# Narrow heads of a latent network: VectorE in source order, returned rows asked for a step earlier, a bias product moved behind the first keys and values

## The chip, the cores and the metric

The kernel runs on one core of a Trainium2 chip. The metric is the device time of one execution in microseconds. The core's engines work side by side, each through its own queue of instructions: TensorE (in profile lines PE, with its weight loads as PEld) multiplies matrices into PSUM, VectorE (DVE) and ScalarE (ACT) work elementwise and empty PSUM, GpSimd (POOL) does small elementwise work and issues gathers, and SyncE (SP) issues most of the other transfers. Instructions of different engines are ordered only by waits on each other's results and by the reuse of buffers.

## The reference, cut to what matters

The reference is a network of four layers. `x` is 16 batches of 64 tokens with 256 features. Each layer adds a cross attention to a context of 1024 keys with 192 features, then a sequence mixer, then a feed-forward part, each on the normalized `x`. The change lies in the cross attention of the second layer, which has 16 heads of only 16 features each ("narrow heads"), and in how it takes over the result of the expert layer ahead of it:

```python
# first layer, feed-forward: two experts of eight for each token
top_w, top_i = top_k(softmax(xt @ gate_w.T), 2)
y = sum over e of comb[:, e] * swiglu(xt, w1[e], w2[e], w3[e])    # comb: top_w, or 0
x = x + y + swiglu(x, sw1, sw2, sw3)

# second layer, cross attention; h = 16 heads, dh = 16
xn = layernorm(x)
q = (einsum('bld,ed->ble', xn, Wq) + bq).reshape(b, l, h, dh)
kv = (einsum('bmc,ec->bme', ctx, Wkv) + bkv).reshape(b, m, h, 2 * dh)
k, v = kv[..., :dh], kv[..., dh:]
att = softmax(einsum('blhd,bmhd->blmh', q, k) / sqrt(dh), axis=2)
out = einsum('blmh,bmhd->blhd', att, v).reshape(b, l, d)
x = x + einsum('bld,ed->ble', out, Wo) + bo
```

## The kernel before, in words

The 1024 tokens lie in SBUF as eight tiles of 128 tokens (`xs`); tile i holds batches 2i and 2i + 1. A framework turns the Python program into one queue for each engine, puts in the waits, and hands out buffers from pools: a tag with `bufs=3` has three buffers that are used in turn, and a fourth allocation waits for the release of the first. As a rule a scheduler chooses the order of each queue by its own estimate of times. Inside `tc.manual_schedule(engines={...})` the engines named keep the order of the source instead.

The stage is `L1_xattn` (from line 867). Ahead of it, the expert layer has written its output rows to a DRAM tensor `ys`. For each token two rows have to be brought back, multiplied by their gates and added to `x`. `carry(i)` (line 1416) does that for tile i: two times it takes a buffer "back" (four of them), has GpSimd gather 128 rows of `ys` (`gather_rows`, line 1414), and has VectorE multiply and add them (line 1423).

`queries(i)` (line 899) is a generator in three steps. The first calls `carry(i)`, normalizes the tile (statistics on VectorE in `norm_tile`, lines 158 to 162, the power -1/2 on GpSimd, line 164, the normalized tile `o` on VectorE, line 904) and has GpSimd add the output bias to `xs` (line 905). The second transposes `o` on TensorE into `hT` (line 908; for tile 0 behind 18 warm-up products). The third computes the queries on TensorE, spreads them on VectorE into `qs` (line 916), and has SyncE copy `qs` to the other half of the partitions (line 921).

`keys_values(b)` (line 926) gives four pieces: keys (TensorE, lines 940 and 942; emptied from PSUM by VectorE, line 945, and ScalarE, line 946), values (lines 954 and 961, emptied through `evict`, line 61 on VectorE or line 63 on ScalarE in turn), keys, values. `biases()` (line 889) computes the row that holds the value bias times the output matrix, plus the output bias: two small VectorE operations (line 892), three products, and a ScalarE copy (line 895).

The loop (line 1039) goes over 64 steps, four groups g of two head pairs for each of 16 batches b. TensorE's order in a step is the source order: it transposes the two exponentiated score tiles `p` of the step before (`keys_first`, line 240) in four groups, whose results are copied from PSUM by VectorE (line 244) and ScalarE (line 242) in turn; then it computes the scores of this step (line 981 by way of line 68); then "early" work; then a piece of the next batch's keys or values; then a step of `queries`, where one is due; then the averages of the step before (line 991); then "late" work. Within `scores`, VectorE takes the maximum of each of the two score tiles (`nmx`, line 228, 128x1024) and ScalarE exponentiates them and sums the rows (line 230).

After the last group of a batch, `own_columns` (lines 1010 and 1011, VectorE, `ym`) picks the columns of each head out of the averages. One step later, as early work, `shares` (line 996) takes the reciprocal of the sums on VectorE (line 999), turns it with a small product on TensorE (line 1003), and ScalarE copies the result (line 1005). For every second batch `weigh` (line 1013) follows another step later, and `project` (line 1021) as late work one step after that.

All PSUM tiles named `misc` share three banks in this stage; the transposes of `p`, keys, values, `shares`, `weigh` and the queries all take theirs from there.

Order of the queues before: at the start (lines 1028 to 1033) TensorE and VectorE are in source order, with `biases()` first. In the loop (line 1034) only TensorE is; VectorE's, ScalarE's, GpSimd's and SyncE's order is the scheduler's.

## Time and profile before

| what | value |
|---|---|
| median of three runs | 2835.01 us (2834.1 to 2840.91) |
| the profiled execution's own time | 2835.53 us |
| its span | 2833.7 us, 46044 instructions |
| TensorE's mean granted clock over the span | 0.98 |
| the last product of the expert layer ends | 425.5 us after the span's start |
| first product of the narrow heads | 429.56 us |
| first scores of the loop | 466.9 us |
| last scores of the loop end | 944.5 us |

A profile row of a timeline gives the start in us, the length in us, the engine, the line, the operation with its tiles and shapes and how many instructions were merged into the row; in brackets stands the idle time ahead of it and what ended it. In a row of waits stand the engine, its tile and line, the engine, tile and line it waited for, and then the total in us, how often, and the longest. A busy share of TensorE is taken from modelled ends of its products, so that a full row does not mean that the array is at its peak. TensorE's granted clock is 1.00 or 0.50 in this trace.

### The profile page before, as it was taken

Reading aid. Unit: us, or ns where it says so; the run is one execution under the profiler, and the core shown is the slowest. Engines: PE = TensorE matmul, PEld = TensorE weight load, DVE = VectorE, ACT = ScalarE, POOL = GpSimd, SP = SyncE. Lnnn points to the kernel's source line nnn. Section 1 sums busy time; section 2 is a strip of 40 time slices with the busy share of each in tenths; the row PEclk is TensorE's granted clock in tenths of the full one; section 3 lists DMA queues with packets and bytes.
Section 4 is the critical chain, followed back from the end, with each engine's and each line's share of the span. In section 5 each row is a group of like instructions: output and inputs, shape, how many; then the busy total and the mean of one; then the engine's idle time right before and its main releaser. Section 6 shows DMA issues by size and latency. Waiting matters only on the chain.

```text
span 2833.7 us, 46044 instructions
## 1 busy us (share of the span) xinstructions
PE 2655.2 (94%) x18778; PEld 1948.1 (69%) x18778; DVE 1403.3 (50%) x2825; ACT 1004.2 (35%) x2114; POOL 311.5 (11%) x429
## 2 busy tenths in 40 slices
PE   7988998999999899989999999998999998998998
PEld 3666894666666688866666666896666665666777
DVE  3665125666666644233434342423344756658692
ACT  2332222555555431222222222122235445455330
POOL 1121323000000112310101000201001000000000
PEclk9999998999999999999999999999999999999999
DMA  9513862111100114801111112463113213121210
GB/s 266 152 53 131 311 245 64 30 27 32 34 28 24 42 38 176 306 25 47 59 58 55 45 49 80 160 239 108 51 49 93 85 48 97 56 76 31 61 45 8
DMA packets 78160, 253.77 MB, mean 90 GB/s; under 512 B 14079, under 2 KB 25882, under 8 KB 68218
## 3 DMA queue, kind: packets, MB, share of 16 engines
q1 hardware_dynamic: 58490, 165.00, 18.6%
q0 software_dynamic: 13312, 80.28, 7.9%
q10 hardware_dynamic: 6144, 5.51, 0.6%
q8 instruction: 149, 2.44, 0.4%
q14 instruction: 65, 0.53, 0.1%
HBM read 233.80 MB, written 14.81 MB: 88 GB/s over the span
## 4 chain that ended last, share of the span: by engine, by line
PE 39%; DVE 9%; ACT 3%; DMA 2%; issue 2%; SPq 1%; POOL 1%; ACTq 0%; DVEq 0%; POOLq 0%
PE sc L516 9%; PE ps_h L68 5%; PE misc L552 4%; PE halves L68 3%; PE ps_t L530 3%; PE misc L68 3%; PE halves L552 2%; PE gu L68 2%; PE misc L547 2%; PE halves L2156 2%; DVE x L2132 2%; DVE nmx L228 1%; PE halves L547 1%; PE po L68 1%; DMA rep<-dus 1%
## 5 line engine op out<-in xcount | busy, mean ns | idle before, releaser
L228 DVE TENSOR_REDUCE nmx<-sc 128x1 f32<-128x1024 f32 x264 | 311.9, 1219 | 221.7 <-PE sc L516 147.6
L230 ACT ACTIVATE p<-sc,nmx 128x1024 f32<-128x1024 f32 x264 | 294.3, 1115 | 308.5 <-DVE nmx L228 308.5
L516 PE MATMUL sc<-ctxT,qp 128*128 128x512 f32 (+1 forms) x1024 | 359.8, 606 | 0.0
L516 PEld LDWEIGHTS sc<-ctxT,qp 128*128 128x128 f32 (+1 forms) x1024 | 140.3, 191 | 156.5 <-issue 153.4
L530 PE MATMUL ps_t<-ident,p 128*128 128x128 f32 x1024 | 140.3, 279 | 39.4 <-ACT pT L533 16.8
L2122 ACT ACTIVATE da<-rep,al 128x252 f32<-128x252 f32 x256 | 115.9, 500 | 133.1 <-DVE x L2132 124.9
L530 PEld LDWEIGHTS ps_t<-ident,p 128*128 128x128 f32 x1024 | 115.6, 142 | 64.1 <-ACT pT L533 20.0
L2132 DVE TENSOR_TENSOR_SCAN x<-da,x 128x512 f32<-128x512 f32 x128 | 153.0, 1222 | 2.7 <-ACT da L2122 1.9
L240 PE MATMUL misc<-ident,p 128*128 128x128 f32 x1024 | 137.1, 279 | 7.2 <-ACT p L230 6.8
L533 ACT COPY pT<-ps_t 128x512 f32<-128x512 f32 x166 | 94.1, 587 | 121.4 <-PE ps_t L530 121.2
L240 PEld LDWEIGHTS misc<-ident,p 128*128 128x128 f32 x1024 | 110.1, 141 | 32.6 <-ACT p L230 15.4
L164 POOL TENSOR_TENSOR ln_rs<-ln_ve,nhalf 128x1 f32<-128x1 f32 x80 | 45.0, 568 | 680.6 <-DVE ln_ve L162 599.1
L552 PE MATMUL halves<-pT,ctx 128*128 128x256 f32 x512 | 119.6, 387 | 0.0
L552 PE MATMUL misc<-pT,ctx 128*128 128x256 f32 x512 | 119.1, 386 | 0.0
L242 ACT COPY pT<-misc 128x512 f32<-128x512 f32 x128 | 75.0, 586 | 109.2 <-PE misc L240 108.7
L68 PE MATMUL ps_h<-r,w 128*128 128x256 f32 x512 | 113.4, 381 | 0.0
L2128 DVE TENSOR_TENSOR x<-rep,bc_rep 128x512 f32<-128x512 f32 x128 | 84.9, 690 | 57.3 <-PE halves L2156 54.4
L244 DVE COPY pT<-misc 128x512 f32<-128x512 f32 x128 | 88.4, 690 | 39.7 <-PE misc L240 28.5
L68 PEld LDWEIGHTS ps_h<-r,w 128*128 128x128 f32 x512 | 96.6, 190 | 15.9 <-issue 2.5
L552 PEld LDWEIGHTS halves<-pT,ctx 128*128 128x128 f32 x512 | 95.0, 191 | 17.4 <-issue 5.6
L552 PEld LDWEIGHTS misc<-pT,ctx 128*128 128x128 f32 x512 | 94.6, 190 | 17.1 <-issue 5.5
L68 PE MATMUL gu<-dT,wa 128*128 128x128 f32 x792 | 94.1, 279 | 7.5 <-DVE dT L61 4.1
(506 smaller groups left out, 4626.1 us busy)
## 6 DMA issues: line engine op xcount, KB each, us to landing
ctx<-in_ctx SPq DMA_DIRECT2D x48, 768.0 KB
ctxT<-in_ctxT SPq DMA_DIRECT2D x48, 512.0 KB
w<-in_L2f_W SPq DMA_DIRECT2D x24, 1024.0 KB
rep<-dus SPq DMA_DIRECT2D x256, 64.0 KB
ctxT<-in_ctxT SPq DMA_DIRECT2D x16, 768.0 KB
ctxT<-in_ctxT SPq DMA_DIRECT2D x96, 128.0 KB
ys<-yb ACTq DMA_DIRECT2D x40, 128.0 KB
bc_rep<-bcs SPq DMA_DIRECT2D x32, 128.0 KB
```

The source lines that it names most:

```text
L68: self.nc.tensor.matmul(out, lhsT, rhs, start=n == 0, stop=n == len(pairs) - 1)
L228: self.nc.vector.tensor_reduce(nmx, sc, AX.X, ALU.max, negate=True)
L230: self.nc.scalar.activation(p, sc, AF.Exp, bias=nmx, accum_out=sums)
L240: self.nc.tensor.transpose(ps[:, u, :], p[:, at : at + 128], self.ident)
L244: self.nc.vector.tensor_copy(pT[:, 0:4, :], ps)
L516: nc.tensor.matmul(sc[u][:, bass.ts(kh, 512)], qp[n][par][rows, h : h + 2, :].rearrange("p h q -> p (h q)"), ctx[0][rows, at], start=n == ...
L530: nc.tensor.transpose(ps[:, t, :], p[:, at : at + 128], self.ident)
L533: nc.scalar.copy(to, ps)
L547: nc.tensor.matmul(o2[cols, :].rearrange("p (u q) -> p u q", u=2), ck[:, t, 128:], pT[:, t, :, cols], start=t == 0, stop=t == NK - 1,)
L552: nc.tensor.matmul(o, ck[:, t, :128], pT[:, t].rearrange("p u q -> p (u q)"), start=t == 0, stop=t == NK - 1)
L2122: nc.scalar.activation(da[:, g, :, 1:], now[j][:, 0, :].rearrange("p (b s) -> p b s", s=S)[:, :, 1:], AF.Exp, scale=al[:, col : col + 1],)
L2132: nc.vector.tensor_tensor_scan(flat, da.rearrange("p g b s -> p (g b s)"), flat, 0.0, ALU.mult, ALU.add)
```

## The change

Three things are changed.

1. The two blocks of fixed order become one, over the whole stage, and VectorE stays in it: in the loop too its queue has the order of the source.
2. `carry` is split. The new `asked(i)` issues the gathers of a tile and gives back a function that does the additions. `carry` calls both at once, as it did. `queries` becomes a generator of four steps: first the gathers alone, then additions, normalization and bias. For tiles 0, 1 and 2 the gathers are asked for at the start; for tiles 3 to 7 in the last step of the batch ahead of the one that adds them (b odd, g = 3).
3. At the start, keys and values of batch 0 come first; `biases()` follows them, then the second step of `queries(0)`, the next keys, the other two steps of `queries(0)`, and the last values.

```diff
         def queries(i):
-            self.carry(i)
+            add = self.asked(i)
+            yield
+            add()
             mv, rs = self.norm_tile(self.xs[:, i, :], 1e-5)
...
         with self.tc.manual_schedule(engines={mybir.EngineType.PE, mybir.EngineType.DVE}):
+            turns = [queries(i) for i in range(3)]
+            next(turns[0])
+            pieces = keys_values(0)
+            pieces[0]()
+            pieces[1]()
             biases()
-            for piece, turn in zip(keys_values(0), (None, *[queries(0)] * 3)):
-                piece()
-                if turn is not None:
-                    next(turn)
-        with self.tc.manual_schedule(engines={mybir.EngineType.PE}):
+            next(turns[0])
+            next(turns[1])
+            pieces[2]()
+            next(turns[0])
+            next(turns[0])
+            pieces[3]()
+            next(turns[2])
             held, work = None, {}
-            one, two = queries(1), queries(2)
+            _, one, two = turns
             ahead = (one,), (one, two), (one, two), (two,)
...
                     elif b % 2 == 0 and g < 3 and b // 2 + 2 < NT:
-                        if not g:
-                            ahead = queries(b // 2 + 2)
+                        next(ahead)
+                    elif b % 2 and g == 3 and b // 2 + 3 < NT:
+                        ahead = queries(b // 2 + 3)
                         next(ahead)
...
     def carry(self, i, room=None, tag="back", bufs=4):
+        self.asked(i, room, tag, bufs)()
+
+    def asked(self, i, room=None, tag="back", bufs=4):
         if self.routed is None:
-            return
-        for n, (at, g) in enumerate(zip(self.routed.at, self.routed.gates)):
+            return lambda: None
+        rows = []
+        for n, at in enumerate(self.routed.at):
             y = self.lp.tile([128, D], F32, tag=tag, bufs=bufs, name="back") if room is None else room[:, n, :]
             self.gather_rows(y, self.ys, at[:, i : i + 1])
-            self.nc.vector.scalar_tensor_tensor(
-                self.xs[:, i, :], y, g[:, i : i + 1], self.xs[:, i, :], ALU.mult, ALU.add
-            )
+            rows.append(y)
+        def add():
+            for y, g in zip(rows, self.routed.gates):
+                self.nc.vector.scalar_tensor_tensor(
+                    self.xs[:, i, :], y, g[:, i : i + 1], self.xs[:, i, :], ALU.mult, ALU.add
+                )
+        return add
```

## The prediction

> **What bounds the kernel now.** I read the page first (busy shares, chain of waits), then busy time by stretch, the waits, and last the timeline of single steps.

> ```profile
> PE 2655.2 (94%) x18778; PEld 1948.1 (69%) x18778; DVE 1403.3 (50%) x2825; ACT 1004.2 (35%) x2114; POOL 311.5 (11%) x429
> PE 39%; DVE 9%; ACT 3%; DMA 2%; issue 2%; SPq 1%; POOL 1%; ACTq 0%; DVEq 0%; POOLq 0%
> ```

> TensorE (PE) is busy 94% of the span and leads the chain. The change touches one stage of twelve, so what counts is whether TensorE waits there. By stretch (length, then busy time of PE, PEld, DVE, ACT, POOL, then TensorE's granted clock, DMA share, GB/s):

> ```profile
> 425.50:466.90 41.40, 28.98 (x109) 15.53 (x109) 18.91 (x58) 3.66 (x7) 23.51 (x31) 0.75 0.29 81
> 466.90:927.00 460.10, 459.12 (x4300) 289.07 (x4302) 300.18 (x402) 250.94 (x452) 4.97 (x8) 1.00 0.11 31
> 453.90:461.90 8.00, 0.07 (x2) 0.04 (x1) 5.37 (x18) 0.00 (x0) 6.43 (x9) 0.63 0.46 139
> 274.70:277.50 2.80, 0.04 (x1) 0.00 (x0) 0.42 (x1) 0.37 (x1) 1.26 (x4) 1.00 1.02 421
> 278.50:281.70 3.20, 3.20 (x17) 3.20 (x16) 0.42 (x1) 0.38 (x1) 0.00 (x0) 0.50 1.04 419
> 2252.90:2255.70 2.80, 0.05 (x4) 0.04 (x2) 2.80 (x5) 2.06 (x5) 0.00 (x0) 1.00 0.16 48
> 2256.00:2262.00 6.00, 6.00 (x51) 5.31 (x48) 0.00 (x0) 1.16 (x4) 0.00 (x0) 1.00 0.00 0
> ```

> The stage's start (425.5 to the first scores at 466.9) loses time; its loop (466.9 to 927) does not: 459.1 of 460.1 us busy. So the start can gain, and in the loop there is nothing to gain and every new wait counts in full. The last four rows are two pauses of TensorE elsewhere: after 2.8 us of rest the clock once fell to 0.50 and once did not. What the start waits for (total, times, longest):

> ```profile
> PE misc L940 <- DVE v L61: 7.9, 1, 7.9
> PE misc L68 <- DVE bv L892: 4.1, 1, 4.1
> ```

> The 7.9 us are keys of batch 1 waiting for a PSUM bank that VectorE (DVE) empties only after it has added and normalized tiles its scheduler drew forward. One step of the loop (start, length, engine, line):

> ```profile
> 522.32 0.20 DVE L999 RECIPROCAL r<-sums 128x8 f32<-128x8 f32 x1 [1.33 <-ACT p L230]
> ...
> 528.74 0.75 DVE L945 TENSOR_SCALAR kT<-misc,vecs 128x512 f32<-128x512 f32 x1 [0.57 <-PE misc L942]
> 529.79 0.48 DVE L1010 TENSOR_SCALAR ym<-o,own 128x256 f32<-128x256 f32 x1 [0.30 <-PE o L991]
> 530.40 0.69 DVE L244 COPY pT<-misc 128x512 f32<-128x512 f32 x1
> 531.00 0.48 DVE L1011 SCALAR_TENSOR_TENSOR ym<-o,own,ym 128x256 f32<-128x256 f32 x1
> 531.14 0.42 PEld L240 LDWEIGHTS misc<-ident,p 128*128 128x128 f32 x4 [0.20 <-DVE pT L244]
> 532.80 0.28 PE L68 MATMUL misc<-ident,r 64*8 64x64 f32 x4
> 532.95 2.36 DVE L228 TENSOR_REDUCE nmx<-sc 128x1 f32<-128x1024 f32 x2 [0.87 <-PE sc L68]
> 533.01 1.99 PE L954 MATMUL misc<-w,ctxT 128*128 128x256 f32 x8
> ```

> See two things. The reciprocal of `shares` ran at 522.3, ten microseconds before the product that reads it (532.80), ahead of the two maxima (532.95 to 535.31). And the fourth group of transposes (531.14) starts 0.05 us after VectorE's first copy of `p` ends: there are three PSUM banks, so that copy is on TensorE's path.

> **The change, part by part.** The order of the changed kernel's queues is known from its compiled form; the times are mine.

> *Start.* TensorE gets its first work (keys, values of batch 0) when the branch ends, about 428.4, not at 429.56. At full clock its work to the first scores is: bias 1.6 (half of 3.1), keys three times 2.97 (441.93 to 444.90), values twice 2.99 (518.51 to 521.50), warm-up 4.2, transposes and queries 1.4; together 22.1. Added waits: VectorE now has `bv` (two at 0.36) behind the copy of `v` (0.68), so the bias product waits 1.5; the `hT` copy 0.6; a bank 0.3. VectorE's chain for tile 0 hides behind keys and warm-up (7 us). The clock was 0.50 for 10.2 us in each of two falls; the first stays, with 3.4 us (another row's length) to 10.2 at half rate, costing 1.7 to 5.1; I take 3.4. First scores: 428.4 + 22.1 + 2.4 + 3.4 = 456.3 against 466.9. **Gain 10.5** (9 to 12). SP only swaps one `qs` copy with a context fetch that is needed a batch later: nothing.

> *Reciprocal behind the maxima.* In source order `scores` comes before `shares`, so the queue is maximum, maximum, reciprocal, in all fifteen batches that have a next one. The product, then the keys or values, averages and transposes behind it in TensorE's queue wait from 532.80 to 535.31 + 0.20 + 0.05 = 535.56: 2.75 us. Fourteen times 2.75; in the last batch, where TensorE waits 1.4 us for `p` anyway, 1.3. **Loss 39.8.**

> *Additions in the loop.* For tiles 3 to 7 VectorE now does, between `kT` and the copy: two additions 0.87, statistics 0.76, a wait for GpSimd's (POOL) power, normalization 0.45, both `ym`. The power stands in GpSimd's queue behind the next gathers that the freed buffers let go (tiles 0 to 5), as it already did once:

> ```profile
> 447.44 0.95 POOL L1414 DMA_INDIRECT back<-ys,route_at  x1 [0.30 <-issue]
> 448.42 0.58 POOL L164 TENSOR_TENSOR ln_rs<-ln_ve,nhalf 128x1 f32<-128x1 f32 x1
> 449.04 0.47 DVE L904 TENSOR_SCALAR o<-xs,ln_mv,ln_rs 128x256 f32<-128x256 f32 x1 [2.20 <-issue]
> ```

> From `kT`'s end, 529.4: first addition 529.9, two gathers with gaps 2.25 to 532.15, power 0.58, normalization to 533.2, `ym` twice to 534.3, copy to 535.0, fourth group 535.04 instead of 531.14: 3.9 us, three times (tiles 3, 4, 5). Without gathers (6, 7): 2.9, twice. For tiles 1 and 2, in batch 0 without `ym` and partly under the exponentials: 3.5 and 2.8. **Loss 23.8.** Everything later in the step waits with it. The gathers of the loop land over 20 us before their addition (a step is 7.2 us, and tile 3 is asked for in step 0 and added in step 8), so asking early costs only GpSimd's order.

> *Both `ym` ahead of the copy* in nine other steps: 0.45 each, **4.0**.

> *Clock.* Twenty-two new pauses. Of ten pauses of 2.2 to 2.8 us in this trace four were followed by a half clock; 3.4 us of it cost 1.7. Ten lone pauses: 10 x 0.4 x 1.7 = 7. Five additions are followed within 1.6 us of work by a `shares` pause, some 6.7 us of rest in 8.3; like 425.5 and 453.9 they should cost one longer fall each, 2.2: 11. **Loss 18**, bounds 0 (as at 2252.9) and 37 (22 x 1.7).
> [...]

> Sum, against the profiled execution's 2835.53 (span 2833.7 and 1.8 around it; the median of the runs is 2835.01): -10.5 + 39.8 + 23.8 + 4.0 + 18 = +75, so **2910 us**.

> **Rivals.**
> 1. *The additions hide* (GpSimd answers sooner, or the gathers don't block it). For: the gathers' own waits may fall elsewhere. Against: VectorE's queue holds the copy behind the normalization whatever GpSimd does. Then 23.8 and the longer falls go: 2835.5 - 10.5 + 39.8 + 4 + 10 = 2879.
> 2. *The clock falls after every pause.* For: 274.7, and 425.5. Against: 2252.9. 2835.5 - 10.5 + 67.6 + 37 = 2930.
> 3. *Faster: the start decides.* The 7.9 us wait is gone and TensorE's order in the loop is the same; if each batch lost under 0.7 us (10.5 over fifteen), the change wins, at best by 10.5: 2825. That needs the reciprocal's place to cost nothing, as it would if the product had slack. For: VectorE is only 65% busy in the loop. Against: 459.1 of 460.1.
> 4. *It doesn't do what it says* (the scheduler keeps its order): the compiled queue shows source order; I give this nothing of its own.

> **How the numbers follow.** Forecast 0.71, rival 1 0.12, rival 2 0.10, rival 3 0.05, no net change 0.02. What a measurement tells from no change is 0.3%, 8.5 us. Own range of the forecast: 2890 (clock 0) to 2925. Taking in rivals 1 and 2: 2876 to 2932. Faster 0.05, same 0.02, slower 0.93.

> **What would show it.** First scores near 456, no 7.9 us wait. In the loop, waits of TensorE's product `misc<-ident,r` for the reciprocal: fifteen, some 40 us; waits of the fourth transposes for VectorE's copy of `p` in the steps with additions; the granted clock below 1.00 in the loop. The prediction is wrong if `shares` doesn't wait, or if TensorE's busy share of the loop stays near 99%.

## The result, and the profile after

| | before | after |
|---|---|---|
| median of four runs | 2835.89 us (2834.10 to 2840.91) | 2903.99 us (2900.50 to 2905.56) |
| the profiled execution: time, span | 2835.53, 2833.7 us | 2905.56, 2903.8 us |
| TensorE's mean granted clock over the span | 0.98 | 0.973 |

The ratio is 1.0236, with a 95% interval from 1.0218 to 1.0253: the change makes the kernel 2.4% slower. 2910 was predicted, in a range from 2876 to 2932.

The page of the changed kernel, busy times and shares of the chain:

```profile
PE 2681.0 (92%) x18778; PEld 1964.0 (68%) x18778; DVE 1404.9 (48%) x2825; ACT 1002.5 (35%) x2114; POOL 311.9 (11%) x429
PE 39%; DVE 8%; ACT 3%; DMA 2%; issue 2%; POOL 1%; SPq 1%; ACTq 0%; DVEq 0%; POOLq 0%
```

TensorE has the same 18778 products and yet 25.8 us more of busy time: products that run longer, not more of them. That is the first sign of the clock. Its share falls to 92% all the same, so it also waits more. The chain's shares say almost nothing, because an average over twelve stages hides one stage.

The stage by stretches. The first row is before, from the first scores to the end of the last output product; the second is the same work after; the third is the start after, from the last product of the expert layer to the first scores (length, then busy time of PE, PEld, DVE, ACT, POOL, then granted clock, DMA share, GB/s):

```profile
466.90:956.47 489.57, 480.87 (x4561) 304.36 (x4560) 317.58 (x423) 265.78 (x480) 5.26 (x11) 1.00 0.10 29
```

```profile
451.16:1026.17 575.01, 510.77 (x4560) 320.83 (x4558) 329.38 (x458) 265.33 (x480) 20.44 (x29) 0.94 0.10 28
422.60:451.20 28.60, 23.91 (x113) 13.41 (x112) 8.83 (x23) 3.66 (x7) 8.42 (x13) 0.94 0.22 61
```

The loop and its end take 575.0 us in place of 489.6: **85.4 more**. TensorE's idle time in it grew from 8.7 to 64.2 (length less busy), 55.5; its busy time by 29.9, at a mean clock of 0.94. The start is shorter: 28.6 us where before had 41.4, **12.9 less** (28.55 and 41.42 unrounded). The stages ahead ended 2.9 us earlier in this execution, and what follows the stage takes 0.3 more. So 85.4 - 12.9 - 2.9 + 0.3 = 69.9, which is the whole difference of the two profiled executions, 70.0, but for rounding.

What TensorE waited for, after, from 422 to 1000 us (total, times, longest):

```profile
PE misc L68 <- DVE r L1001: 41.7, 13, 4.9
PE misc L68 <- ACT p L230: 7.2, 2, 4.5
PE misc L240 <- ACT pT L242: 4.6, 16, 0.3
PE misc L942 <- PEq L1413: 2.9, 1, 2.9
PE misc L68 <- ACT v L63: 1.1, 1, 1.1
```

The first row is the forecast's main one: the product of `shares` waits for the reciprocal (line 1001 after, 999 before). Two of its waits are booked to ScalarE's `p` instead, which ended at about the same time (second row); together 15 pauses and 48.9 us. The 2.9 us are the rest ahead of the stage's first product, where before had 4.1. The 7.9 us wait of the start is gone, and the wait for `bv` is now 1.1 us, booked to a copy of `v`.

A step with nothing but the reciprocal, timeline of after:

```profile
566.62 2.36 DVE L228 TENSOR_REDUCE nmx<-sc 128x1 f32<-128x1024 f32 x2 [1.26 <-PE sc L68]
568.89 0.19 DVE L1001 RECIPROCAL r<-sums 128x8 f32<-128x8 f32 x1
569.14 0.28 PE L68 MATMUL misc<-ident,r 64*8 64x64 f32 x4 [2.57 <-DVE r L1001]
569.35 3.15 PE L956 MATMUL misc<-w,ctxT 128*128 128x256 f32 x8
```

VectorE takes both maxima first, then the reciprocal; TensorE rests 2.57 us. Such a pause, with nothing else that makes VectorE late, is called a lone pause below. The eight products behind it take 3.15 us, where the same row took 1.99 before: for most of that time they run at half clock (granted clock 0.62 from 569.3 to 572.5 us). A step in which a tile is added, too:

```profile
521.14 0.75 DVE L947 TENSOR_SCALAR kT<-misc,vecs 128x512 f32<-128x512 f32 x1 [0.57 <-PE misc L944]
521.81 0.99 DVE L1441 SCALAR_TENSOR_TENSOR xs<-back,route_g,xs 128x256 f32<-128x256 f32 x2
...
523.88 0.66 PE L240 MATMUL misc<-ident,p 128*128 128x128 f32 x4 [0.29 <-ACT pT L242]
523.99 0.95 POOL L1424 DMA_INDIRECT back<-ys,route_at  x1 [0.30 <-DVE ln_ve L162]
...
524.95 0.59 POOL L164 TENSOR_TENSOR ln_rs<-ln_ve,nhalf 128x1 f32<-128x1 f32 x1
525.58 0.41 DVE L906 TENSOR_SCALAR o<-xs,ln_mv,ln_rs 128x256 f32<-128x256 f32 x1 [1.91 <-POOL ln_rs L164]
...
526.82 1.28 DVE L244 COPY pT<-misc 128x512 f32<-128x512 f32 x2
528.02 2.35 DVE L228 TENSOR_REDUCE nmx<-sc 128x1 f32<-128x1024 f32 x2
...
530.53 0.38 PE L68 MATMUL misc<-ident,r 64*8 64x64 f32 x4 [4.92 <-DVE r L1001]
530.84 3.78 PE L956 MATMUL misc<-w,ctxT 128*128 128x256 f32 x8
```

The gather does stand ahead of the power in GpSimd's queue, and VectorE loses 1.91 us to it, as forecast. But the last transposes (523.88) do not wait for VectorE's copy at 526.82: they go on after 0.29 us, in a bank that ScalarE empties. VectorE's lateness is carried through its queue into the maxima and the reciprocal, and comes out as one pause of 4.92 us.

### The profile page after: what moved, and what is told of

The parts are those of the page before. It is cut to its first block, busy times and chain, and to the rows that moved or that the text cites. A ratio compares the mean times of both kernels' runs of the same rounds, so it can differ in the third digit from the quotient of the medians.

```text
span 2903.8 us, 46042 instructions
## 1 busy us (share of the span) xinstructions
PE 2681.0 (92%) x18778; PEld 1964.0 (68%) x18778; DVE 1404.9 (48%) x2825; ACT 1002.5 (35%) x2114; POOL 311.9 (11%) x429
## 4 chain that ended last, share of the span: by engine, by line
PE 39%; DVE 8%; ACT 3%; DMA 2%; issue 2%; POOL 1%; SPq 1%; ACTq 0%; DVEq 0%; POOLq 0%
PE sc L516 9%; PE ps_h L68 4%; PE misc L552 4%; PE halves L68 3%; PE ps_t L530 3%; PE misc L68 3%; PE halves L552 3%; PE gu L68 2%; PE misc L547 2%; PE halves L2176 2%; DVE x L2152 1%; PE halves L547 1%; DVE nmx L228 1%; PE po L68 1%; DMA rep<-dus 1%
## 5 line engine op out<-in xcount | busy, mean ns | idle before, releaser
L228 DVE TENSOR_REDUCE nmx<-sc 128x1 f32<-128x1024 f32 x264 | 311.7, 1218 | 218.8 <-PE sc L516 145.3
L230 ACT ACTIVATE p<-sc,nmx 128x1024 f32<-128x1024 f32 x264 | 294.0, 1114 | 337.7 <-DVE nmx L228 337.7
L530 PE MATMUL ps_t<-ident,p 128*128 128x128 f32 x1024 | 140.7, 280 | 40.2 <-ACT pT L533 17.3
L240 PE MATMUL misc<-ident,p 128*128 128x128 f32 x1024 | 139.3, 280 | 11.0 <-ACT p L230 5.4
L240 PEld LDWEIGHTS misc<-ident,p 128*128 128x128 f32 x1024 | 110.8, 141 | 37.8 <-ACT p L230 13.5
L164 POOL TENSOR_TENSOR ln_rs<-ln_ve,nhalf 128x1 f32<-128x1 f32 x80 | 45.0, 568 | 820.2 <-DVE ln_ve L162 667.5
L68 PE MATMUL ps_h<-r,w 128*128 128x256 f32 x512 | 113.4, 381 | 0.0
L244 DVE COPY pT<-misc 128x512 f32<-128x512 f32 x128 | 86.9, 689 | 47.4 <-PE misc L240 35.6
L68 PEld LDWEIGHTS ps_h<-r,w 128*128 128x128 f32 x512 | 96.7, 190 | 15.8 <-issue 2.5
L1424 POOL DMA_INDIRECT back<-ys,route_at x34 | 37.0, 1089 | 654.9 <-DVE xs L1441 237.8
```

The lines of the kernel that those rows point to most:

```text
L68: self.nc.tensor.matmul(out, lhsT, rhs, start=n == 0, stop=n == len(pairs) - 1)
L228: self.nc.vector.tensor_reduce(nmx, sc, AX.X, ALU.max, negate=True)
L230: self.nc.scalar.activation(p, sc, AF.Exp, bias=nmx, accum_out=sums)
L240: self.nc.tensor.transpose(ps[:, u, :], p[:, at : at + 128], self.ident)
L244: self.nc.vector.tensor_copy(pT[:, 0:4, :], ps)
L530: nc.tensor.transpose(ps[:, t, :], p[:, at : at + 128], self.ident)
```

## The experiments

Each kernel ran beside the kernel before on the same chip; a ratio is to that kernel's median there (2834.89 us for e1 to e4, 2833.40 for e5 to e7, 2839.05 for e8 to e10). "Loop" is the stretch of 489.6 us above, read from each profile in the same way; idle is its length less TensorE's busy time. The last column is the time in the loop with a granted clock of 0.50; a fall is the start of such a stretch. Outside the loop, too, the profiled executions differ by some us (the stages ahead ended between 420.3 and 430.5 us, what follows the loop took 1871 to 1883), so parts of the loop are compared in the traces.

| run | median us | ratio to before, 95% interval | loop us | TensorE idle in it | of it at half clock |
|---|---|---|---|---|---|
| before | | 1 | 489.6 | 8.7 | 2.2 |
| after | 2903.99 | 1.0236 (1.0218 to 1.0253) | 575.0 | 64.2 | 63.6 |
| e1 reciprocal early | 2840.79 | 1.0028 (1.0012 to 1.0044) | 509.5 | 24.0 | 4.8 |
| e2 additions apart | 2889.73 | 1.0203 (1.0186 to 1.0221) | 560.1 | 54.6 | 49.0 |
| e3 both | 2830.82 | 0.9987 (0.9976 to 0.9998) | 501.3 | 17.3 | 4.8 |
| e4 fill | 2885.49 | 1.0191 (1.0172 to 1.0211) | 550.8 | 28.0 | 10.2 |
| e5 `ym` split | 2826.25 | 0.9971 (0.9959 to 0.9983) | 496.3 | 13.2 | 3.4 |
| e6 tiles 1, 2 moved | 2820.46 | 0.9953 (0.9938 to 0.9968) | 493.7 | 11.5 | 3.1 |
| e7 bias first | 2823.99 | 0.9965 (0.9952 to 0.9978) | 494.3 | 11.5 | 5.3 |
| e8 asked with addition | 2908.81 | 1.0253 (1.0230 to 1.0277) | 573.5 | 64.2 | 60.1 |
| e9 more row buffers | 2906.53 | 1.0240 (1.0213 to 1.0267) | 568.1 | 61.7 | 54.5 |
| e10 small fill | 2889.78 | 1.0185 (1.0161 to 1.0209) | 555.1 | 45.1 | 23.9 |

(e4 and e10 have added products, which count as busy.)

### e1: the reciprocal early

```diff
+        def reciprocals(sums):
+            r8 = self.lp.tile([128, 8], F32, tag="r8", bufs=2, name="r8")
+            nc.vector.reciprocal(r8, sums)
+            return r8
-        def shares(sums, par, rT):
-            r8 = self.lp.tile([128, 8], F32, tag="r8", bufs=2, name="r8")
-            nc.vector.reciprocal(r8, sums)
+        def shares(r8, par, rT):
...
                     own_columns(o, ym, par)
-                    work[k + 1, "early"] = [lambda hs=hs, par=par, rT=rTs[i % 2]: shares(hs, par, rT)]
+                    work[k + 1, "early"] = [lambda r8=reciprocals(hs), par=par, rT=rTs[i % 2]: shares(r8, par, rT)]
```

> The changed kernel with one thing undone: VectorE takes the reciprocal of `shares` right behind both `ym` of the step before, ahead of the next copies of `p` and the next two maxima; its product stays where it is. Theory (the reciprocal's place is the main loss): the 14 pauses ahead of the `shares` product go, nine of 2.57 us and 2.57 of each of the five longer ones, 36.0 together, and 1.3 in the last batch, and with them the falls of the clock (13 windows of half rate, 54.4 us, worth at most 27): from 2904 to 2845 to 2855, the upper end if the five steps with additions keep their 2.35 us (4.92 less 2.57) and a fall each. Rival (VectorE is late by itself in those steps, the reciprocal only shows it): the waits move to the copies of `p` or to `p`, 2885 to 2904.

Measured: 2840.79 us, a little below the expected 2845. The loop lost 65.5 of its 85.4 us of excess, by one instruction of 0.19 us in each batch, put in another place. TensorE's waits from 455 to 915 us:

```profile
PE misc L68 <- DVE r L1000: 6.1, 5, 1.6
PE misc L240 <- ACT pT L242: 4.7, 16, 0.3
PE misc L956 <- DVE pT L244: 1.6, 6, 0.7
```

The lone pauses are gone. The five steps with additions still wait for the reciprocal, but 1.2 us on average and not 2.35, and no half clock follows them. The rival falls: by itself VectorE's lateness costs 6.1 us in these five steps; most of the loss is the reciprocal's place in the queue.

### e2 and e3: the additions apart, and both

```diff
-        def queries(i):
+        def queries(i, apart=False):
             add = self.asked(i)
             yield
             add()
+            if apart:
+                yield
             mv, rs = self.norm_tile(self.xs[:, i, :], 1e-5)
+            if apart:
+                yield
...
-                    elif b % 2 == 0 and g < 3 and b // 2 + 2 < NT:
-                        next(ahead)
-                    elif b % 2 and g == 3 and b // 2 + 3 < NT:
-                        ahead = queries(b // 2 + 3)
+                    elif b % 2 == 0 and g in (1, 2) and b // 2 + 2 < NT:
+                        next(ahead)
+                    elif b % 2 and b // 2 + 3 < NT:
+                        if not g:
+                            ahead = queries(b // 2 + 3, apart=True)
                         next(ahead)
```

e3 has the edits of e1 and e2 together.

> The changed kernel with the additions of tiles 3 to 7 taken apart: asked for in the first step of the odd batch, added in the second, statistics in the third, normalized in the fourth, so that no step holds them all and GpSimd's power has a step's time; the reciprocal stays behind the maxima. Theory (additions cost only what lies above the lone pause): five pauses of 4.92, 4.92, 4.92, 3.75, 4.50 become 2.57, which is 10.2 us less, and one to three windows of half clock shorter, 2 to 5: from 2904 to 2889 to 2893. My prediction's size (23.8 and 11 of clock) would give about 2870. Rival (additions fully hidden): 2904.

> The two edits together (reciprocal early, additions apart); the start, the bias and VectorE's order of the rest are those of the changed kernel. Theory (these two orders are the whole loss of the loop, and the start's gain of 13 stands): 2835.5 - 13 = 2822, faster than the kernel before, TensorE busy over 99% of the loop and full clock in it. With my prediction's own term of 4.0 for both `ym` ahead of the copy: 2826. Rival (the order by source costs something else in the loop): 2835 or more.

e2 came out at 2889.73, where the theory had 2889 to 2893 and my prediction's size for the additions 2870: taken alone they are worth 14.9 us of the loop (575.0 less 560.1), not 35. With e1 already in, they are worth 8.2 more (509.5 less 501.3).

e3 is faster than the kernel before, but only by 0.13%, 2830.82 where I expected 2822 to 2826. So something else in source order costs the loop 11.8 us. What TensorE still waits for in e3, 455 to 915 us:

```profile
PE misc L240 <- ACT pT L242: 4.6, 16, 0.3
PE misc L960 <- DVE pT L244: 0.7, 1, 0.7
PE misc L946 <- DVE pT L244: 0.6, 1, 0.6
```

These are the three largest rows; the other five are of 0.2 to 0.5 us. The first row is one wait of 0.29 us for each batch: the fourth group of transposes (not the third, as the expectation for e5 says) waits for a bank. The others are single waits in the first steps. That gave the next two runs.

### e4 and e10: the pauses filled

```diff
-            pr = self.misc([40, S])
+            room = self.misc([128, 128])
+            self.warm(room, 9)      # e10: 4
+            pr = room[:40, :S]
```

`warm` issues products of the identity with ones; what they write is overwritten by the product of `shares`. Each is two instructions in the trace (x18 for nine).

> The changed kernel with nine products of the identity (0.275 us each, 2.48) ahead of the product of `shares`, in the bank it overwrites: TensorE is busy in the pauses, which stay as long. It separates the clock from the wait. Theory (the half clock after a pause costs its length times a half, 1.7 us for each window of 3.4): the eight windows behind lone pauses go, 13.6, and perhaps those behind the five longer pauses in part: from 2904 to 2882 to 2891. Rival (the half clock costs nothing, its step has slack later): 2904. Rival (the fill delays its product): above 2905.

> As the fourth run, with four products (1.1 us) for nine (2.48) ahead of the product of `shares`: a lone pause of 2.57 keeps 1.47 us of rest. In the nine traces so far the half clock starts on a grid of 3.413 us, each time to within 0.014 us; of 100 stretches of that grid at full clock in which TensorE was busy less than 0.40 all were followed by a half one, of 205 with 0.5 to 0.6... 22 of 163, above 0.6 some 1 in 130. Theory (the busy share of a grid stretch decides): with 1.47 us of rest a stretch stays over 0.56 busy, so next to none of the ten lone pauses costs a half clock: 2885 to 2888, as good as the full fill. Rival (any rest of over about a microsecond can bring it, at random): falls behind half of the lone pauses, 2893 or more.

In a step with the reciprocal alone, the fill leaves VectorE's order and the wait for the reciprocal as they are, and keeps the array busy meanwhile. In four of the five steps with additions the fill itself first waits for a bank that VectorE's late copy of `p` empties (6.6 us in all). The median, 2885.49 us, is inside e4's expected range. The loop gets 24.2 us shorter (550.8 for 575.0), and the half clock shrinks from 63.6 to 10.2 us. So of the loop's 85.4 us some 24 (what the fill gave back) to 30 (what TensorE's busy time had grown by) are clock and the rest is waiting. (By the ratios, 1.0191 for 1.0236, the whole kernel kept some 13 us of the 24; what follows the loop took 5.8 us more in this trace.) The same step as at 569.14 above, timeline of e4:

```profile
560.53 2.27 PE L75 MATMUL misc<-ones,ident 128*128 128x128 f32 x18
...
563.17 0.28 PE L68 MATMUL misc<-ident,r 64*8 64x64 f32 x4 [0.36 <-DVE r L1001]
563.38 1.99 PE L956 MATMUL misc<-w,ctxT 128*128 128x256 f32 x8
```

The row of line 956 takes 1.99 us again. And of e10, with less than half of the fill:

```profile
570.79 1.16 PE L75 MATMUL misc<-ones,ident 128*128 128x128 f32 x8
573.43 0.28 PE L68 MATMUL misc<-ident,r 64*8 64x64 f32 x4 [1.48 <-DVE r L1001]
573.64 1.99 PE L956 MATMUL misc<-w,ctxT 128*128 128x256 f32 x8
```

This rest of 1.48 us is followed by full clock (1.99 us once more for line 956). None of the nine lone pauses in e10's loop brought a half clock; the four falls it has follow steps with additions. Beside the kernel before e10 is 1.85% slower and e4 1.91%, the same within their intervals. e10's time, 2889.78 us, lies between the two expectations and decides nothing; its loop is 4.3 us longer than e4's, with 13.7 us more of half clock, all of it behind steps with additions. For the lone pauses none in nine is what the theory expected, next to none, and not the rival's fall behind half of them.

### e5 and e6: the rest of the source order

e5 puts `ym`'s second operation and the reciprocal between VectorE's two copies of `p`; e6 also takes tiles 1 and 2 out of the first steps. The first diff is against e3, the second against e5; both show the main lines only, and their comments are added here.

```diff
-                        pT.append(self.keys_first(p[u]))
+                        pT.append(self.keys_first(p[u], *([] if u or rest is None else [rest])))
+                    rest = None
...
-                    own_columns(o, ym, par)
+                    y = own_columns(o, ym, par)           # the first operation only
+                    box = []
+
+                    def rest(o=o, y=y, hs=hs, box=box):
+                        own_rest(o, y)                     # the second
+                        box.append(reciprocals(hs))
```

```diff
                     if not b:
-                        for turn in ahead[g]:
-                            next(turn)
+                        next(ahead)                        # queries(1, apart=True)
+                    elif b == 1 and not g:
+                        next(ahead)
+                        ahead = queries(2, apart=True)
+                        next(ahead)
...
-                    elif b % 2 and b // 2 + 3 < NT:
+                    elif b % 2 and b // 2 + 2 < NT:
                         if not g:
-                            ahead = queries(b // 2 + 3, apart=True)
+                            ahead = queries(b // 2 + 2, apart=True)
```

> The kernel of the third run (reciprocal early, additions apart) with `ym`'s second operation and the reciprocal put behind VectorE's first copy of `p`, as the kernel before had it (`ym`, copy, `ym`, copy). In the third run's trace the third transposes of the step wait 16 times 0.29 us for ScalarE's bank, 4.6 in all: VectorE's copy comes late by both `ym`. Theory (that order is what these waits are): they go, the loop gets 4.6 us shorter (501.3 to 496.7), 2826. Rival (they are ScalarE's own): 2831, no change.

> The kernel of the fifth run with tiles 1 and 2 taken out of the first two steps: tile 1 is added, measured, normalized and transposed one step each in batch 0, tile 2 in batch 1 as the later tiles are. Theory (the third run's gaps in the first four steps, 0.59, 0.50, 0.69, 0.48 and two of 0.2 to 0.3, are these additions): loop 3 us shorter again, about 493 against 489.6 before; the start's gain of 13 to 14.5 stands in full: 2835 - 13 + 3.5 = 2822 to 2826, a version faster than both kernels. Rival (those gaps are the first exponentials, which the kernel before had hidden by its late start): no change against the fifth run.

Both came as expected: the loop 496.3 (496.7 expected), then 493.7 (493); e6's time is a little below the 2822 to 2826 expected. In e5 the sixteen waits for ScalarE's bank have become two, in all 0.5 us:

```profile
PE misc L240 <- ACT pT L242: 0.5, 2, 0.3
```

That bank was only the place where VectorE's late copy showed. e6 is **faster than the kernel before by 0.47%** (0.32 to 0.62%), and 2.8% faster than the changed one. It keeps the change's start and its fixed order of VectorE, but an order that is laid out for TensorE:

```profile
452.28:945.95 493.67, 482.15 (x4561) 305.04 (x4560) 328.39 (x458) 265.44 (x480) 20.31 (x29) 1.00 0.11 32
```

Its loop is 4.1 us longer than that of the kernel before, and it gives that back three times over at the start.

### e7: the bias product first

```diff
             pieces = keys_values(0)
+            biases()
             pieces[0]()
             pieces[1]()
-            biases()
```

> The kernel of the sixth run with the bias product ahead of the first keys again, as in the kernel before; all else stays. It tells the two parts of the start's gain apart. Theory (the bias product's place gives TensorE its first work 1.2 us earlier, 2.9 for 4.07 us of rest, and a half clock of 3.4 for 10.2 us, 3.4 of time, less the 1.06 us wait for `bv`): 3.5 us slower than the sixth run, and the other 9 to 10 us of the gain are the 7.9 us wait. Rival (all of the gain is the 7.9 us wait): no change. Rival (the half clock hurts more): 5 or more slower.

Measured: medians 3.5 us apart, as expected, but the intervals of the two ratios overlap, so the time alone does not tell. In the traces it is 28.5 us from the expert layer's last product to the first scores in e7 and 26.8 in e6, 1.7 more. e7's first rows:

```profile
430.20 1.10 PE L68 MATMUL misc<-w,bv 128*128 128x256 f32 x4 [3.86 <-DVE bv L892]
431.23 0.74 PE L68 MATMUL misc<-w,ones 1*128 1x256 f32 x2
431.90 3.59 PE L946 MATMUL misc<-ctxT,w 128*128 128x512 f32 x4
```

The wait for `bv` is back, and one half clock of 3.4 us follows it (the row of line 946 takes 3.59 us, where e6's first takes 1.96), not the 10.2 of the kernel before. But TensorE's idle time at the start is the same in both, 4.6 us in e7 and 4.5 in e6, since e6 rests 2.7 us ahead of its first product and 1.1 ahead of the bias product. The 1.7 us are that half clock alone (busy 23.9 and 22.3 us), and e6 merely has none. With the keys first, as in the change, the half clock comes too in six of ten kernels (after, e1, e2, e8, e9, e10), whose starts took 28.5 to 29.1 us; the four without it (e3 to e6) took 26.7 to 27.1. So e7's 28.5 us is no longer than a keys-first start with the same half clock: the bias product's place is worth nothing that shows in the traces, and the 3.5 us between the medians are not explained by it. The rival that all of the gain comes with the 7.9 us wait stands.

e7 keeps 13.0 us of gain at the start over the kernel before with the bias product in its old place. In the change the start's 12.9 are 7.75 us less of idle time (12.44 to 4.69: the 7.9 us wait) and 5.1 us less of busy time (29.0 to 23.9: less work at half clock). The kernel before had two stretches of 10.2 us at half clock there, the second from 455.9 us on, within its 7.9 us wait. VectorE's additions of all tiles, which the scheduler had drawn ahead of the start's copies, are out of the way in every version; which of the other edits at the start matter was not tried one by one.

### e8 and e9: the returned rows

```diff
-                        next(ahead)
-                    elif b % 2 and g == 3 and b // 2 + 3 < NT:
-                        ahead = queries(b // 2 + 3)
+                        if not g:
+                            ahead = queries(b // 2 + 2)
+                            next(ahead)
                         next(ahead)
```

That is e8; e9 has `add = self.asked(i, bufs=10)` instead.

> The changed kernel with the returned rows of tiles 3 to 7 asked for in the step of their addition again, not a step ahead; VectorE and TensorE keep the changed kernel's order. Theory (GpSimd's queue is the scheduler's own: the gathers stand there as soon as their buffers come free, whatever the source says, so this part of the change does nothing): 2904, within 0.3%. Rival (asking late makes the additions wait for the landing, 2.9 us from issue): up to 5 x 2.9 = 14 us and some falls of the clock more, 2918 to 2925.

> The changed kernel with ten buffers for returned rows in place of four: the gathers of tiles 3 and 4 no longer wait for the buffers of tiles 1 and 2, and in the steps of tiles 3, 4 and 5 no gather stands ahead of the power in GpSimd's queue. Theory (two gathers ahead of the power make those three pauses 4.92 and not 3.75 like tile 6's): 1.2 us less three times, and where a half clock of 6.8 us becomes 3.4, 1.7 less: 2904 to 2895 to 2901. Rival (the gathers hide behind VectorE's own work): 2904.

e8 shows no effect of asking a step ahead: 1.0253 with an interval that overlaps the changed kernel's, and a loop of 573.5 for 575.0. GpSimd's order is not the source's; in both traces the last three pairs of gathers go out in the same steps, behind the additions that free their buffers (at 522.6, 596.9 and 671.6 us in after, 525.3, 599.8 and 674.5 in e8).

e9 is a miss in time and a hit in the trace. Its three pauses are 3.7 us and not 4.9, the power has no gather ahead of it, and VectorE waits 0.66 us for it where it had waited 1.91:

```profile
530.53 0.55 POOL L164 TENSOR_TENSOR ln_rs<-ln_ve,nhalf 128x1 f32<-128x1 f32 x1 [52.64 <-DVE ln_ve L162]
531.12 0.41 DVE L906 TENSOR_SCALAR o<-xs,ln_mv,ln_rs 128x256 f32<-128x256 f32 x1 [0.66 <-POOL ln_rs L164]
...
536.06 0.28 PE L68 MATMUL misc<-ident,r 64*8 64x64 f32 x4 [3.68 <-DVE r L1001]
```

The loop is 7.0 us shorter than the changed kernel's. The ratio to before shows nothing of it, and its interval (1.0213 to 1.0267, 15 us wide) is too wide to tell the expected 3 to 9. In the profiled execution the 7.0 us are lost outside the loop: the stages ahead ended at 430.5 us and not at 422.6, the start took 0.5 us more and what follows the loop 2.2 more. In the other eleven traces the stages ahead ended between 420.3 and 428.0, so whether the larger pool has a part in that stays open.

## Why the prediction was right, and where it was not

The direction, the cause and nearly the sum were right: the terms for the loop added up to 85.6 us (39.8 + 23.8 + 4.0 + 18) and the loop lost 85.4. That close a sum is luck, since two terms were wrong by some 10 us in opposite directions. The shown terms add up to some 84.5.

| step of the prediction | predicted | shown |
|---|---|---|
| start | -10.5 | -12.9 |
| reciprocal behind the maxima | +39.8 | +37.0: fourteen times 2.57 (36.0) and 1.0 in the last batch (2.66 less the 1.62 that such a step rests there anyway) |
| additions in the loop | +23.8 | some +13: 10.2 in the five merged pauses, some 2.6 in the first four steps (single waits of 0.2 to 0.7; e6 gives 2.6 back) |
| both `ym` ahead of the copy | +4.0 | +4.6, sixteen times 0.29 and not nine times 0.45 |
| clock | +18 | +29.9 more of busy time; 24 came back with the fill |

**Start.** The step mis-sized is the half clock: 3.4 us of it were there, as predicted, but cost 1.7 us, half its length (TensorE busy 23.9 us with it in e7, 22.3 without in e6), and not the 3.4 that I took. The wait for `bv` was 1.1 and not 1.5. That the 7.9 us wait would go was right: idle time there fell by 7.75 us. e7 shows that the gain doesn't rest on the bias product's new place. And the 3.4 us of half clock came in six of the ten kernels that start with the keys; four have none.

**Reciprocal.** The mechanism and the size of the pauses were right (2.57 us each for 2.75); e1 shows it by taking only that away. It was also the lever on the other terms, which the sum could not show: with the reciprocal early, a part of the lateness of the additions hides as well (waits of 6.1 us are left of 10.2), and the clock stays up (4.8 us of half clock in e1's loop for 63.6). Undone alone, e1's part gives back 65.5 us and e2's 14.9; undone together, 73.7, and not the sum of 80.4. These terms, which share a queue, don't add.

**Additions.** This is the step that failed. I let the late copy of `p` delay the fourth group of transposes by 3.9 us and then counted the reciprocal's 2.75 on top. In the changed kernel that group takes a bank that ScalarE empties (0.29 at 523.88), so it runs on, and VectorE's lateness meets TensorE only at the next place where TensorE reads from VectorE, the reciprocal. There it lengthens a pause that exists already: 4.92 less 2.57 is 2.35 us for tiles 3, 4 and 5, 1.2 for tile 6, 1.9 for tile 7, where the statistics of the next stage get between (a timeline row of GpSimd's power shows it waiting for `ln_mv` of line 1598). That gathers in GpSimd's queue would cost some 1.2 us a tile was right (e9). I had taken the waiting place from the trace of before, where that group starts behind VectorE's copy (531.14); but the bank that it gets is not the same in the two kernels.

**Clock.** The step that failed is the rate of 0.4. Thirteen of the fourteen pauses ahead of the loop's end were followed by a half clock, in stretches of 3.4 or 6.8 us. The ten pauses in the trace of before, four of them with a fall, gave no rate for this loop. A difference between them was in that trace: three of the four falls follow a 3.413 us stretch in which TensorE was busy 0.26 to 0.33, while the six pauses without a fall leave no stretch below 0.42; the fourth fall, at 56.6 us, follows one of 0.52. Rival 2 had nearly the right rate (its 22 x 1.7 = 37 against 29.9) and the wrong waits; rival 1 had the additions too small; rival 3 falls with e1.

## What to carry to other kernels

Putting one engine's queue in source order moves every instruction that the scheduler had drawn forward, and the cheapest one can cost most: a 0.19 us reciprocal, put behind two maxima, held the busiest engine for 2.57 us or more in each of fifteen batches. Before fixing an order, list for each engine what the bottleneck reads from it next, and put those instructions first; then the same fixed order is a gain (e6). And where several things make one engine late, count the wait once, at the next place where the bottleneck reads from it (4.92 us here), and not at each place on the way (3.9 and 2.75).

## What the runs showed of the hardware

Lone pauses of the same length differed by their place on the grid. In the loop of after, eight of the nine, of 2.57 or 2.60 us, had 2.02 us or more in one stretch and were followed by a fall; the ninth, at 930.66, lay 1.19 and 1.38 us in two stretches and was not. In e10 the rests of 1.48 to 1.51 us are at most 0.44 of a stretch, and none of nine was followed by a fall. The counts are of what happened in these traces, and what sets the clock is not shown; only e4 and e10 filled the pauses and left the waits.

**What a fall costs.** In after's loop 61.4 more us of half clock went with 29.9 more us of busy time, 0.49 us for each, beside a granted clock of 0.50 in them.
